# Squares of four head pairs folded by transfers and summed in one group of matmuls

## The chip, the cores and the metric

The kernel runs on one core of a Trainium2 chip. The metric is device time in microseconds (us) of one execution. A profiled execution lasts a little longer than its recorded span, since some work lies around the span.

## What is computed

A layer norm over 2048 tokens of 512 values is followed by two branches whose product is added to the input. The change touches the first one, an attention over four lags. Cut to what matters:

```python
q = _causal_dwconv(_silu(x @ Wq), conv_q_w)      # k and v likewise; 16 heads of 128
q = q * cos + rot_half(q) * sin                  # k likewise
q = q / jnp.maximum(jnp.linalg.norm(q, axis=-1, keepdims=True), 1e-12)
k = k / jnp.maximum(jnp.linalg.norm(k, axis=-1, keepdims=True), 1e-12)
for s in range(4):
    attn = jnp.einsum('bshd,bshd->bsh', q, _lag(k, s)) * scale
    out = out + (attn * sigmoid(_lag(a, s) * b))[..., None] * _lag(v, s)
```

Then out is divided by its root mean square over all heads, gated by silu(x @ Wz), and multiplied by Wout. The second branch is a feed-forward net with weights reduced to their signs. For the change only one thing has to be seen: per token and head, the kernel needs the sum over 128 channels of q squared and of k squared (the norms), and of q times k at four lags (the dots). Channels lie on partitions, so such a sum is a matmul by a matrix of zeros and ones.

## The kernel before, in words

Tokens come in four blocks of 512 (index b, 0 to 3), the 16 heads in eight pairs (index p, 0 to 7). A pair has 256 channels, laid out as two slices j of 128 partitions; in each slice partitions 0 to 63 belong to one head and 64 to 127 to the other.

`step(p, b)` (line 663) is the unit of work. For pair p it makes queries, keys and their products of block b+1, and values, gates and output of block b. TensorE does in it 8 matmuls each for q, k, v and z (`project`, line 339), and in every even p the output projection of the two pairs before (`output_projection`, line 616: four token chunks of four matmuls, the first two of each chunk for the earlier pair). Steps with b = -1 make block 0, with the feed-forward net's work in between. So blocks 1, 2 and 3 of the products are made in the steps with b = 0, 1 and 2.

In `products` (line 416), for pair p: ScalarE squares both slices of q and k into two tiles sq0 and sq1 (128 x 2 x 512, 512 KB each), and one accumulating DMA of GpSimd's queue adds sq1 to sq0 (line 435). VectorE multiplies q by the lagged k into tiles pr (128 x 4 x 512, 1 MB). In blocks 1 to 3 the dots of two pairs are brought into one tile. In an even p the second slice is added by DMA (line 452), then partitions 32 to 63 are added to 0 to 31, and 96 to 127 to 64 to 95, by two accumulating DMAs (line 469). In an odd p the pair's own tile goes into the free half of the tile of the pair before: two plain copies (line 472) and two accumulating DMAs onto them (line 473). The four dots of two pairs are then one group of four matmuls (`sum_dots`, line 494) with the matrix of_heads.

The squares are not brought together so. `sum_squares` (line 484) makes two matmuls for each pair (k and q) with of_head: even pairs write partitions 0 to 63 of the PSUM tile squares, odd pairs 64 to 127, so two pairs are four matmuls on four different groups of 32 columns. It is called at p = 2, 4 and 6 of a step between the second and third chunk of the output projection (`strips`, line 695) together with `sum_dots` of the last two pairs, and once more at p = 0 of the next block, before `norms` (line 505). `norms` adds both halves of the tile squares.

In `weighted` (line 569) the tiles te0 and te2 (one buffer each) hold coefficients times v; the output o stays in te0. In steps with b = 0 the squares of o go to te2 and from there to DRAM by a DMA of GpSimd's queue (line 599); in later steps they go through a free part of xnT. The tiles bc (three buffers) bring coefficients from DRAM by DMAs of SyncE's queue. `gated_output` (line 607) makes oz, which the output projection reads.

What goes through the wrapper InOrder (all TensorE and VectorE work, much of ScalarE's, the stores of line 599, the loads of bc) keeps its program order. DMAs issued by nc.gpsimd and nc.sync are placed into the queues of GpSimd and SyncE by the framework's scheduler when the kernel is built; from then on each queue runs in its order, and an instruction that waits holds up all behind it. GpSimd's queue carries the folds of sq and pr, the stores of parts of the output (lines 637 and 639), the accumulations of the next layer norm (line 241) and the stores of line 599. SyncE's carries all weights.

The tile pool holds sq0 in three buffers taken in turn, and sq1 in one.

Of the kernel before, what the change touches and what calls it, by code (L numbers as in the profile page):

```python
# [38 lines left out]
F32 = mybir.dt.float32  # L39
F32R = mybir.dt.float32r  # L40
AF = mybir.ActivationFunctionType
ALU = mybir.AluOpType
PSUM = bass.MemoryType.PSUM

P = 128
# [3 lines left out]
D = 128  # L49
# [4 lines left out]
NP = H // 2  # L54
TB = 512
# [26 lines left out]
def recurrent_layer(ctx: ExitStack, tc: tile.TileContext, a: dict, out: bass.AP):  # L82
    nc = tc.nc
# [12 lines left out]
    of_head = const.tile([P, NP, LW], F32, name="of_head")  # L96
# [3 lines left out]
    of_heads = const.tile([P, NP // 2, LW], F32, name="of_heads")  # L100
# [25 lines left out]
    qks = qk.enter_context(tc.tile_pool(name="qks", bufs=1))  # L126
# [174 lines left out]
    def load(pool, n, p, b):  # L301
        w = pool.tile([P, KC, 2 * P], F32, tag="w", name=f"w{n}{p}_{b}", bufs=3)
        loads["by"].dma_start(w, a[f"w{n}"][p])
        weights[n] = w
# [16 lines left out]
    def sum_with_halo(pool, name, p, b):  # L321

        if name in to_keep:
            to_keep.pop(name)()
        t = pool.tile([P, 2, HALO + TB], F32, tag=name, name=f"{name}_{p}_{b}", bufs=1)
        act.copy(t[:, :, 0:HALO], kept[name][:, p])
        if b < NTB - 1:
            to_keep[name] = lambda: act.copy(kept[name][:, p], t[:, :, TB : TB + HALO])
        return t
# [35 lines left out]
    def raw_of(pool, n, p, b, bufs=2, raw=None):  # L365

        raw = raw or with_halo(pool, f"r{n}", "raw", bufs, p, b)
        project(n, p, b, raw[:, :, HALO:])
        keep_halo(f"r{n}", raw, p, b)
        return raw  # L370

    def convolve(i, p, raw, to):

        for j in range(2):
            nc.scalar.mul(to[:, j, :], raw[:, j, HALO:], conv_w[:, i, p, j, LAGS - 1 : LAGS])  # L375
            for w in range(LAGS - 2, -1, -1):
                dve.scalar_tensor_tensor(
                    to[:, j, :],
                    raw[:, j, w : w + TB],
                    conv_w[:, i, p, j, w : w + 1],  # L380
                    to[:, j, :],
                    ALU.mult,
                    ALU.add,
                )

    banks = {}

    dots_due = []
    squares_due = []
    outputs_due = []  # L390

    def queries(p, b):

        if p or b:
            load(qks, "q", p, b)
        q = qks.tile([P, LAGS, 2, TB], F32, tag="q", name=f"q_{p}_{b}", bufs=1)
        q0 = q[:, LAGS - 1]
        convolve(0, p, raw_of(qks, "q", p, b), q0)
        return q

    def turn(q):
# [8 lines left out]
        for s in range(2, LAGS):  # L410
# [2 lines left out]
                q[:, at], q[:, at + 1], turns[:, 3:4], q[:, at + 2], ALU.mult, ALU.subtract  # L413
            )

    def products(p, b, q, between=None, beside_k=None):

        n = f"_{p}_{b}"
        if p or b:
            load(qks, "k", p, b)  # L420
        q0 = q[:, LAGS - 1]
        raw = raw_of(qks, "k", p, b)
        if p == 0:
            sum_squares(p)
        k = sum_with_halo(qks, "k", p, b)
        convolve(1, p, raw, k[:, :, HALO:])
        if between:
            between()
        turn(q)

        sq = [qks.tile([P, 2, TB], F32, tag=f"sq{j}", name=f"sq{j}" + n, bufs=3 - 2 * j) for j in range(2)]
        for j in range(2):
            act.activation(sq[j][:, 0], q0[:, j], AF.Square)
            act.activation(sq[j][:, 1], k[:, j, HALO:], AF.Square)
        nc.gpsimd.dma_start(sq[0], sq[1], accum_op=ALU.add)
        squares_due.append((p, sq[0]))
        if beside_k:
            beside_k()

        def product(to, j, lo, hi):  # L440

            k0 = k[:, j, lo : lo + TB]
            k_lags = bass.AP(k0.tensor, k0.offset, [k0.ap[0], [1, hi - lo], k0.ap[1]])
            dve.tensor_tensor(to, q[:, lo:hi, j, :], k_lags, ALU.mult)

        pr = qks.tile([P, LAGS, TB], F32, tag="pr", name="pr0" + n, bufs=2)
        product(pr, 0, 0, LAGS)
        if not b or p % 2 == 0:
            pr1 = qks.tile([P, LAGS, TB], F32, tag="pr", name="pr1" + n, bufs=2)
            product(pr1, 1, 0, LAGS)  # L450
            if b:
                nc.gpsimd.dma_start(pr, pr1, accum_op=ALU.add)
            elif p < NP - 1:
                dve.tensor_tensor(pr, pr, pr1, ALU.add)
        else:

            product(q[:, :, 1], 1, 0, LAGS)
            dve.tensor_tensor(pr, pr, q[:, :, 1], ALU.add)
        if not b:

            prs = [pr, pr1] if p == NP - 1 else [pr]
            dots_due.append([p, prs, of_head[:, p], p == NP - 1, True])
            return


        for h in range(0, P, D // 2):
            first, second = slice(h, h + D // 4), slice(h + D // 4, h + D // 2)
            if p % 2 == 0:
                nc.gpsimd.dma_start(pr[first], pr[second], accum_op=ALU.add)
            else:  # L470
                both = dots_due[-1][1][0]
                nc.gpsimd.dma_start(both[second], pr[first])
                nc.gpsimd.dma_start(both[second], pr[second], accum_op=ALU.add)
        if p % 2 == 0:
            dots_due.append([p, [pr], of_heads[:, p // 2], p == NP - 2, False])
        else:
            dots_due[-1][-1] = True

    def add(to, s, heads, src, start, stop):

        rows = to[LW * s : LW * s + LW, :]
        pe.matmul(rows, heads, src, start=start, stop=stop, tile_position=(0, LW * s))

    def sum_squares(last):


        while squares_due and squares_due[0][0] != last:
            p, sq = squares_due.pop(0)
            if p == 0:
                banks["squares"] = sums.tile([P, TB], F32, tag="squares", name="squares")  # L490
            for i in (1, 0):
                add(banks["squares"], 2 * (p % 2) + 1 - i, of_head[:, p], sq[:, i, :], p < 2, p >= NP - 2)

    def sum_dots():

# [48 lines left out]
    def squares_of_o():  # L544
        while o_due:
            o_due.pop(0)()
# [116 lines left out]
    def step(p, b, beside_q=None, beside_k=None):  # L663

        at = b >= 0
        change = p == 0 and at
        q = queries(p, b + 1)
        squares_of_o()
        if x_due:
            x_due.pop()()  # L670
        rv = with_halo(vs, "rv", "raw", 1, p, b) if p == b == 0 else None
        if beside_q:
            beside_q()
        if change and b:
            sum_squares(p)
            norms(b)
        due = bool(dots_due) and dots_due[0][-1]
        if change and not b:

            def beside_k():  # L680
                norms(b)
                norms_in_rows(b)

        products(p, b + 1, q, (lambda: norms_in_rows(b)) if change and b else None, beside_k)
        if z_due:
            z_due.pop()()
        if at:
            load(vs, "v", p, b)
            raw = raw_of(vs, "v", p, b, 1, rv)
        if first_due:  # L690
            first_due.pop()()
        if at:
            v = values(p, b, raw)

        def strips():

            if p and p % 2 == 0:
                sum_squares(p)
            if p == NP - 2 and b + 2 < NTB:
                gate_products(b + 2)  # L700
            if p == 1 and not at:
                gate_products(0)
            if due:
                sum_dots()

        z = []
        z_of = lambda: z.append(gates_of_output(p, b))

        early = p == 2 and b == 0
        if early:  # L710
            load(vs, "z", p, b)
            z_of()

        output_projections(strips if p % 2 == 0 or due else None)
        if change:
            coefficients(b)
        if at:
            if not early:
                load(vs, "z", p, b)
            load_wo(p, b)  # L720
            out_of = lambda: gated_output(p, b, weighted(p, b, v), z[0])
            if change:
                z_due.append(z_of)
                first_due.append(out_of)
            else:
                if not early:
                    z_of()
                out_of()
        if p == (3 if at else 2):
            load_gate(b + 1)  # L730
        elif p == (4 if at else 3):
            gate()
        if b + 2 < NTB:
            if p < TC:
                statistics(b + 2, p)
            if p == (TC if at else TC - 1):
                centre(b + 2)
            elif p == 5:
                divide(b + 2)
# [226 lines left out]
    with tc.tile_pool(name="ff", bufs=1, side="right") as ff:  # L966
# [75 lines left out]
        for b in range(1, NTB):  # L1042
# [31 lines left out]
            if b == last:  # L1074

                scale, silu, by_y, plus_x = ends(b, pf)
                n = len(hids)
# [97 lines left out]
```

## Time and profile before

| what | us |
|---|---|
| median of three runs | 1400.17 (1399.67 to 1402.85) |
| the profiled execution | 1400.38 |
| its span | 1398.6 |
| VectorE busy in it | 1179.3 |
| ScalarE busy in it | 671.3 |
| GpSimd busy in it | 236.1 |

The profile's page lists busy time of each engine, groups of instructions with their mean duration, and a chain of work followed back from the end. The trace can be asked for any stretch of the span: the timeline of one engine gives start, duration, operation, output and inputs of merged instructions and, in brackets, the idle time before the first of them with what ended it. Of float32 matmuls there are two records each, so that four matmuls are listed as x8. The issue of a DMA is a short record on its queue's engine; the time to landing is given apart. Times of the timelines count from the span's start. Windows give the mean busy share of the 16 DMA engines.

The times of GpSimd's transfers by the trace, over the whole span: the folds of sq (32 of 512 KB) land in 6.7 us in the median, the 72 small transfers of pr (256 KB) in 6.9 us, the 12 large ones (1 MB) in 10.7 us.

### The profile page before, as it was taken

The numbers are of one execution on the slowest core, as the hardware profiler recorded it, in microseconds if no ns is written. First come the engines' busy times: TensorE is split into PE (matmuls) and PEld (weight loads), VectorE is DVE, ScalarE is ACT, GpSimd is POOL, SyncE is SP. The second block draws the span as 40 slices with busy tenths as digits, with TensorE's granted clock in tenths as the row PEclk, the third lists the DMA queues.
The fourth block names the chain that finished last, engine by engine and source line by source line (L and its number), as shares of the span: only waits on it lengthen the run. The fifth ranks groups of instructions, "written<-read, shape, count | busy, mean of one in ns | idle before, by whom it ended". The sixth has DMA issues, their size and how long they took to land.

```text
span 1398.6 us, 12500 instructions
## 1 busy us (share of the span) xinstructions
PE 1387.6 (99%) x3962; PEld 689.6 (49%) x3962; DVE 1179.3 (84%) x1183; ACT 671.3 (48%) x1309; POOL 236.1 (17%) x317
## 2 busy tenths in 40 slices
PE   9999999999999999999999999999999999999998
PEld 6555544444444444444444444444444444578886
DVE  7998989999898989998999999989884987337454
ACT  7566656546454564565545544545442433222122
POOL 2222111112213121113131112111111122200000
PEclk9999999999999999999999999999999999999999
DMA  9979577888988789889986897888849999654020
GB/s 315 332 171 211 129 200 166 228 203 197 231 199 186 167 167 242 212 211 196 212 186 159 171 251 186 207 181 182 176 92 207 262 233 237 142 204 136 24 90 30
DMA packets 104985, 263.40 MB, mean 188 GB/s; under 512 B 17812, under 2 KB 18324, under 8 KB 100568
## 3 DMA queue, kind: packets, MB, share of 16 engines
q0 software_dynamic: 36672, 108.02, 40.0%
q1 hardware_dynamic: 68248, 154.58, 37.1%
q8 instruction: 32, 0.52, 0.2%
q14 instruction: 33, 0.27, 0.1%
HBM read 159.77 MB, written 52.45 MB: 152 GB/s over the span
## 4 chain that ended last, share of the span: by engine, by line
PE 87%; DVE 7%; DMA 3%; ACT 1%; issue 1%; SPq 0%; DVEq 0%; ACTq 0%
PE pq L76 14%; PE pk L76 14%; PE po L76 14%; PE pz L76 13%; PE pv L76 12%; PE ph L76 8%; PE pf L76 8%; DVE q L76 2%; DVE te L76 2%; DMA wk<-in_wk_dram 1%; DVE v L76 1%; PE dots L76 1%; DMA bc<-co_dram 1%; PE squares L76 1%; DVE k L76 1%
## 5 line engine op out<-in xcount | busy, mean ns | idle before, releaser
L76 PE MATMUL pq<-xnT,wq 128*128 128x512 f32 (+1 forms) x528 | 226.1, 580 | 0.6 <-ACT rk L310 0.6
L76 PE MATMUL pk<-xnT,wk 128*128 128x512 f32 x512 | 225.3, 592 | 0.8 <-DMA wk<-in_wk_dram 0.8
L76 PE MATMUL pz<-xnT,wz 128*128 128x512 f32 x512 | 225.2, 592 | 0.5 <-ACT rv L363 0.5
L76 PE MATMUL po<-wo,oz 128*128 128x512 f32 x512 | 225.6, 595 | 0.0
L76 PE MATMUL pv<-xnT,wv 128*128 128x512 f32 x512 | 225.2, 592 | 0.0
L76 DVE TENSOR_TENSOR te<-v,bc 128x2048 f32<-128x2048 f32 x64 | 143.8, 2288 | 33.8 <-ACT v L76 15.8
L76 DVE SCALAR_TENSOR_TENSOR k<-rk,conv_w,k 128x512 f32<-128x512 f32 x192 | 141.7, 751 | 31.6 <-ACT k L375 27.1
L76 PEld LDWEIGHTS pq<-xnT,wq 128*128 128x128 f32 x528 | 99.0, 189 | 123.4 <-issue 115.1
L76 PEld LDWEIGHTS po<-wo,oz 128*128 128x128 f32 x512 | 96.2, 190 | 126.5 <-issue 117.1
L76 PEld LDWEIGHTS pz<-xnT,wz 128*128 128x128 f32 x512 | 96.6, 189 | 124.0 <-issue 119.2
L76 PEld LDWEIGHTS pv<-xnT,wv 128*128 128x128 f32 x512 | 96.6, 189 | 123.8 <-issue 120.2
L76 PEld LDWEIGHTS pk<-xnT,wk 128*128 128x128 f32 x512 | 96.5, 189 | 121.7 <-issue 119.6
L76 DVE SCALAR_TENSOR_TENSOR q<-rq,conv_w,q 128x512 f32<-128x512 f32 x192 | 141.5, 749 | 17.4 <-ACT q L375 10.6
L76 DVE SCALAR_TENSOR_TENSOR v<-rv,conv_w,v 128x512 f32<-128x512 f32 x192 | 141.3, 750 | 6.4 <-ACT v L375 1.9
L76 DVE SCALAR_TENSOR_TENSOR q<-q,turns 128x1024 f32<-128x1024 f32 (+1 forms) x128 | 127.3, 1015 | 4.9 <-ACT q L76 2.6
L76 DVE TENSOR_TENSOR pr<-q,k 128x2048 f32<-128x2048 f32 x52 | 117.3, 2287 | 0.9
L76 DVE CAST hid_hi<-hid 128x512 fp32r<-128x512 f32 x52 | 22.4, 430 | 89.7 <-ACT hid L785 89.7
L785 ACT ACTIVATE hid<-ph,up_scale 128x512 f32<-128x512 f32 x64 | 43.6, 685 | 108.6 <-PE ph L76 108.0
L363 ACT ACTIVATE rq<-pq 128x512 f32<-128x512 f32 x62 | 36.9, 596 | 98.2 <-PE pq L76 98.1
L633 ACT COPY part<-po 128x512 f32<-128x512 f32 x64 | 37.0, 580 | 87.8 <-PE po L76 87.7
L76 PE MATMUL ph<-xs_hi,up 128*128 128x512 f32 x192 | 76.8, 400 | 0.0
L76 PE MATMUL ph<-xs_lo,up 128*128 128x512 f32 x192 | 75.6, 394 | 0.0
(154 smaller groups left out, 1747.2 us busy)
## 6 DMA issues: line engine op xcount, KB each, us to landing
bc<-co_dram SPq DMA_DIRECT2D x128, 256.0 KB
pr<-pr POOLq DMA_DIRECT2D x72, 256.0 KB, 6.9
wq<-in_wq_dram SPq DMA_DIRECT2D x32, 512.0 KB
wk<-in_wk_dram SPq DMA_DIRECT2D x32, 512.0 KB
sq<-sq POOLq DMA_DIRECT2D x32, 512.0 KB, 6.7
wv<-in_wv_dram SPq DMA_DIRECT2D x32, 512.0 KB
wz<-in_wz_dram SPq DMA_DIRECT2D x32, 512.0 KB
wo<-in_wo_dram SPq DMA_DIRECT2D x32, 512.0 KB
```

What stands on the lines that cost most here:

```text
L76: return self.tc.keep_in_program_order(getattr(self.engine, op)(*args, **kwargs))
L363: nc.scalar.activation(to[:, j, :], pp, AF.Silu)
L633: nc.scalar.copy(part, po)
L785: nc.scalar.activation(hid, ph, AF.Relu, scale=scale)
```

## The change

The folding of a pair's tile is moved into a helper `beside`, which serves pr as before, and now sq too, for pairs 0 to 3 of blocks 1 to 3. There, after sq1 has been added to sq0, an even pair's tile is folded by two accumulating DMAs of 128 KB; an odd pair's tile goes into the free half of the tile of the pair before by two plain copies and two accumulating DMAs of 128 KB. Pairs 0 to 3 then take two entries in place of four, both summed at p = 4 with of_heads; the call at p = 2 is left out in the steps with b >= 0. Pairs 4 to 7 and block 0 are summed as before. The three buffers of sq0 have tags of their own, and each pair is given one by hand.

```diff
+    def beside(p, of_pair, both):
+        for h in range(0, P, D // 2):
+            first, second = slice(h, h + D // 4), slice(h + D // 4, h + D // 2)
+            if p % 2 == 0:
+                nc.gpsimd.dma_start(of_pair[first], of_pair[second], accum_op=ALU.add)
+            else:
+                nc.gpsimd.dma_start(both[second], of_pair[first])
+                nc.gpsimd.dma_start(both[second], of_pair[second], accum_op=ALU.add)
...
-        sq = [qks.tile([P, 2, TB], F32, tag=f"sq{j}", name=f"sq{j}" + n, bufs=3 - 2 * j) for j in range(2)]
+        place = (2, 0, 1, 0, 0, 2, 1, 0)[p] if b else p % 3
+        sq = [
+            qks.tile([P, 2, TB], F32, tag=tag, name=f"sq{j}" + n, bufs=1)
+            for j, tag in enumerate((f"sq_{place}", "sq1"))
+        ]
...
         nc.gpsimd.dma_start(sq[0], sq[1], accum_op=ALU.add)
-        squares_due.append((p, sq[0]))
+        if not b or p >= NP // 2:
+            squares_due.append((p, sq[0], of_head[:, p], p % 2, p < 2, p >= NP - 2))
+        else:
+            beside(p, sq[0], squares_due[-1][1] if p % 2 else None)
+            if p % 2 == 0:
+                squares_due.append((p, sq[0], of_heads[:, p // 2], p // 2, True, False))
...
-            p, sq = squares_due.pop(0)
+            p, sq, heads, odd, start, stop = squares_due.pop(0)
...
-                add(banks["squares"], 2 * (p % 2) + 1 - i, of_head[:, p], sq[:, i, :], p < 2, p >= NP - 2)
+                add(banks["squares"], 2 * odd + 1 - i, heads, sq[:, i, :], start, stop)
...
-            if p and p % 2 == 0:
+            if p and p % 2 == 0 and not (at and p == 2):
                 sum_squares(p)
```

How the built queues differ: TensorE has 12 matmuls less and is otherwise in the same order, VectorE's order is the same. GpSimd has 36 DMAs more, each set right behind the sq fold of its pair and so ahead of that pair's transfers of pr. On SyncE two weight loads stand earlier: wk of pair 4 of block 1 stands ahead of the second half of bc of pair 3, the loads of the gate and one of x, where it stood behind them; wv of pair 4 in the step with b = 1 likewise. ScalarE has a few small moves in the same places.

More of the change, by code (lines that the diff above doesn't have):

```diff
@@ L463, in products @@
             return
[L466 to L473, printed above, removed]
+        beside(p, pr, dots_due[-1][1][0] if p % 2 else None)
         if p % 2 == 0:
```

## The prediction

> **What bounds the kernel now.** I read the page's busy times first, then the chain of waits, then timelines of single engines around the edit.
>
> ```profile
> span 1398.6 us, 12500 instructions
> PE 1387.6 (99%) x3962; PEld 689.6 (49%) x3962; DVE 1179.3 (84%) x1183; ACT 671.3 (48%) x1309; POOL 236.1 (17%) x317
> ```
>
> TensorE idles 11 us in all. The timeline of PE has no gap between 335.7 and 1089 us, so a matmul taken out there is time won, and a wait put in is time lost. Step p=4, b=0, where pairs 0 to 3 of block 1 will be summed:
>
> ```profile
> 342.60 7.03 PE L76 MATMUL po<-wo,oz 128*128 128x512 f32 x16
> 349.56 1.06 PE L76 MATMUL squares<-sq,of_head 128*32 128x512 f32 x8
> 350.44 1.04 PE L76 MATMUL dots<-pr,of_heads 128*32 128x512 f32 x8
> 351.42 7.13 PE L76 MATMUL po<-wo,oz 128*128 128x512 f32 x16
> ```
>
> See the starts, not the durations: the four square matmuls take 350.44 - 349.56 = 0.88 us of PE, since they run side by side on four column groups.
>
> The last stall before the gapless stretch, by the chain and by PE's timeline:
>
> ```profile
> 299.01 2.30 DVE te L76
> 301.31 0.02 issue
> 301.33 7.01 DMA bc<-co_dram
> ...
> 308.40 20.25 DMA wk<-in_wk_dram
> ```
> ```profile
> 328.79 7.11 PE L76 MATMUL pk<-xnT,wk 128*128 128x512 f32 x16 [0.80 <-DMA wk<-in_wk_dram]
> ```
>
> And GpSimd's queue in step p=3, b=0:
>
> ```profile
> 318.73 0.86 POOL L435 DMA_DIRECT2D sq<-sq  x1 [8.96 <-ACT sq L76]
> 328.42 1.04 POOL L472 DMA_DIRECT2D pr<-pr  x2 [8.82 <-DVE pr L76]
> 335.72 0.79 POOL L473 DMA_DIRECT2D pr<-pr  x1 [6.27 <-DMA pr<-pr]
> 339.74 0.78 POOL L473 DMA_DIRECT2D pr<-pr  x1 [3.23 <-DMA pr<-pr]
> ```
>
> By the times to landing the sq fold took 9.4 us, the two last transfers 12.1 and 9.5 us: the dots' operand is whole at 339.74 + 9.5 = 349.2, and PE reads it at 350.44. That is 1.2 us of slack, and the edit puts new transfers ahead of these four lines.
>
> **Matmuls removed.** Twelve at a mean of 592 ns would be 7.1 us, but they overlap. One group costs 349.56 to 350.44 = 0.88; at p=6 the starts of squares, ab and dots (420.29, 421.18, 422.04) give 0.89 and 0.86. One group of two goes in each of three blocks: 3 x 0.87 = 2.6 us. The dots group stays at p=2, so the switch between tile shapes around it (7.13 in place of 7.03 for the next po) stays too.
>
> **Loads moved.** On SyncE's queue wk of pair 4 now stands ahead of bc, gates and x. Its buffer comes free when pq of pair 3 ends (about 300.4), so it issues some 8 us earlier than 308.40; even with 20.25 us to land it is there at 321 for a use at 328. The 0.80 us stall goes. What is late next is oz of pair 3: VectorE has no idle time from 263 to 342, oz ends at 342.07, and PE wants it two matmuls into the po of 342.60, at about 344.3. Slack 2.2 us, of which 0.87 + 0.80 would be used. bc gets the extra wait of one issue and is read 30 us later: nothing. In b=1 wv moves from 585.86 to at the earliest 578.6 (the end of pz), and bc behind it waits for VectorE until 580.95 anyway: nothing.
>
> **Transfers added.** 36 DMAs of 128 KB, 12 per block. Their issue is 0.5 to 0.8 us each by L472/L473, about 25 us on a GpSimd busy 236 us: no bound. What counts is that copy and accumulate wait for landings, with everything behind them held.
>
> *Even pairs.* In p=2 the fold of 286.97 lands in 4.6 us at 291.6, the two half folds are out by 293.2, and the pr fold waits for VectorE until 294.80: nothing. In p=0 of block 1 the same (213.78 + 6.9 = 220.7, pr at 226.04). In p=0 of block 2 498.83 + 6.6 makes pr 1.7 us late, with the next sq at 523.42 free again.
>
> *p=1, b=0.* sq fold 242.06, lands in 7.7: 249.8. Two copies of 128 KB: no row has them; 256 KB took 4.9 here, I take 4.3 (bounds 3 and 5): 254.2 and 254.8. Accumulates out by 255.9. pr copies at 256.0 in place of 252.22, 5.0 to land, pr accumulates out by 262.8, so the store of te2 (queued behind) issues at 262.9 in place of 261.93. With its 7.3 us it lands at 270.2; VectorE rewrites te2 at 269.86. The added 0.5 MB comes on top: the software queue's 108 MB took 40% of the span, 5.2 us a MB, so up to 2.6 us where the DMA engines are full (shares 1.05, 1.03, 1.11 from 246 to 264). VectorE waits 0.3 to 3 us, I take 1.5. PE's po of 277.70 wants oz only two matmuls in and has 2.3 us: hidden. But VectorE stays late to 342, where only 2.2 - 1.67 = 0.6 was left, so PE waits 0.9 there.
>
> *p=3, b=0.* This is the term that decides. sq squares 1.5 late (they follow VectorE): fold 320.2, +9.4 = 329.6. Copies 5 us (bounds 3.5, the 256 KB rows of the later blocks, and 8.8, this step's own row): 335.2. Accumulates out at 336.1. pr copies 336.2 and 336.7 in place of 328.42; they land in 3.5 to 8.8, I take 6, since 336 to 342 has a DMA share of 0.64: 342.7. Last accumulate issues at 343.5; landing 7 to 12.1, I take this step's 9.5, as 342 to 360 is full (1.07 to 1.10): 353.0. The optimistic ends give 348, the pessimistic 358. PE arrives at 350.44 - 1.67 + 0.9 = 349.7 and waits 3.3 us. Against before, dots start 353.0 - 350.44 = 2.6 us later. Behind them stand the rest of po and the whole gapless stretch; nothing takes it back. What GpSimd has queued behind (layer-norm accumulations, part stores) has its users 20 us or more away. ScalarE rewrites the buffer of pair 3's squares at 347.64, which the accumulates leave at about 344: 3 us to spare.
>
> *Blocks 2 and 3.* p=3, b=1: 599.98 + 9.9 = 609.9, copies 3.6, accumulates out 615, pr copies 615.1 in place of 610.13, +3.6, accumulates out 620.1, +6.9 = 627; dots at 634.56. 7 us free. b=2 (882.71, +9.5; dots 918.68) is alike, and p=1 of both leaves 5 us or more. Nothing, and each keeps its 0.87.
>
> **A rule against the row.** The Trainium skill, "DMA: Bandwidth & Descriptors", section "Anatomy of one DMA", puts a transfer at about 2.0 us plus its bytes over 436 GB/s: 3.2 us for the sq fold, 2.3 for each of 128 KB, 2.6 for 256 KB. The p=3 chain would then be 320.2 + 3.2 + 2.3, pr copies at 328.4 as now, and the dots' operand there at 335: no wait, and the change would win the whole 3.4 us. The rows say 9.4 and 12.1 for the same kinds, because the engines are shared with the loads of weights. I take the rows.
>
> **Sum** on the profiled execution (1400.38; the median is 0.21 below, inside the runs' spread): +2.6 at the dots of block 1 (with the first group and the 0.80 swallowed by it) - 2 x 0.87 = +0.9, so 1401.3.
>
> **Rivals.**
> 1. *The wait eats the gain* (above): operand whole at 350 to 354.8, 1398.9 to 1403. Chance 0.45.
> 2. *The transfers are hidden*: they land by 349.7, since wk's 512 KB now moves before 320 and frees the engines from 318 on. Then -2.6 - 0.8 = -3.4, 1397.0, up to 1398.8 with some wait for VectorE. For it: landings of 3.5 in later blocks. Against: 9.4 to 10.0 for every sq fold of odd pairs but one of 7.7 and one of 8.8. Chance 0.23, 0.14 of it below 1397.4.
> 3. *Slower: GpSimd's chain in p=3, b=0 at its slow rows.* From a landing after 354.8 the loss (4.4 - 1.7) is over 0.2%; at 357 it is 6.6 - 1.7 = +4.9, 1405.3. For it: 8.8 and 12.1 were seen in this very step, and a late VectorE delays its start. Chance 0.24.
> 4. *Traffic*: 4.7 MB more at 5.2 us is 24 us of full DMA time, and weight loads elsewhere come late; a few stalls like that of 0.80 would give 1404. Against: no such wait now after 335. Chance 0.08.
>
> That the matmuls saved count in full (7.1 us, 1393) contradicts the starts above; 0.01 or less.
>
> About 0.2% (2.8 us) is what a measurement of this kernel can tell from no change. Faster by more: 0.14 (part of 2). Slower: 0.24 + 0.06 + 0.05 of case 1's upper end. Same: 0.51. The range 1397.0 to 1406.0 leaves out the ends of 2 and of 3; case 1's own is 1398.9 to 1403.0.
>
> **What would show it.** In the profile after: squares gone at p=2 and po to po there about 0.98 us apart; no wait for wk at 328; pr copies of pair 3 some 8 us after the sq fold's landing; PE waiting before the dots of pairs 2 and 3 of block 1, named as a DMA of pr; none in blocks 2 and 3, whose spacing of p=2 shrinks by 0.87. I am wrong if the dots of block 1 wait for nothing, if blocks 2 or 3 wait as well, or if the store of te2 doesn't hold up VectorE near 270 yet oz is late.

## The result and the profile after

The changed kernel takes 1423.07 us in the median of five runs (1422.68 to 1424.81), the kernel before in the same session 1401.58 (1399.67 to 1402.85): 1.0157 times as long, 95% interval 1.0143 to 1.0172. The profiled execution lasted 1423.62 us, so 23.2 more than the one of before. The forecast was 1401.3, its range ended at 1406.0.

The page of the changed kernel, first the span with the busy times, then the first line of the chain that ended last:

```profile
span 1421.8 us, 12490 instructions
...
PE 1390.8 (98%) x3938; PEld 690.0 (49%) x3938; DVE 1179.6 (83%) x1183; ACT 671.3 (47%) x1309; POOL 261.7 (18%) x353
...
PE 74%; DMA 10%; DVE 9%; issue 3%; ACT 2%; POOL 1%; SPq 0%; DVEq 0%; POOLq 0%; ACTq 0%
```

TensorE has 24 records (12 matmuls) less and yet is busy 3.2 us longer; its idle time has gone from 11 to 31 us. The waits of TensorE, with us in total, times, and the longest:

```profile
PE dots L76 <- DMA pr<-pr: 11.8, 2, 10.8
PE po L76 <- DVE oz L76: 6.2, 1, 6.2
PE pz L76 <- ACT rv L363: 2.4, 1, 2.4
```

None of the first two stood in the profile before; the third had 0.5 us there. TensorE's timeline in the steps p=2 and p=4 with b=0 puts the two long waits into block 1:

```profile
278.03 1.88 PE L76 MATMUL po<-wo,oz 128*128 128x512 f32 x4
286.10 8.12 PE L76 MATMUL po<-wo,oz 128*128 128x512 f32 x12 [6.19 <-DVE oz L76]
294.14 1.06 PE L76 MATMUL dots<-pr,of_heads 128*32 128x512 f32 x8
...
358.59 1.05 PE L76 MATMUL squares<-sq,of_heads 128*32 128x512 f32 x4 [0.39 <-DMA sq<-sq]
370.41 1.94 PE L76 MATMUL dots<-pr,of_heads 128*32 128x512 f32 x8 [10.76 <-DMA pr<-pr]
372.27 7.71 PE L76 MATMUL po<-wo,oz 128*128 128x512 f32 x16
```

The squares are gone at p=2 (only the dots stand between the chunks of po), and the dots of p=4 start at 370.41 where they started at 350.44. In blocks 2 and 3 one wait of 1.01 us is left (the dots of block 2's pairs 2 and 3, at 656.34). Why block 1 is late, GpSimd's queue tells, first p=1, then p=3, both b=0:

```profile
251.51 1.03 POOL L424 DMA_DIRECT2D sq<-sq  x2 [7.96 <-DMA sq<-sq]
258.34 0.79 POOL L425 DMA_DIRECT2D sq<-sq  x1 [5.80 <-DMA sq<-sq]
...
260.15 1.28 POOL L424 DMA_DIRECT2D pr<-pr  x2
267.30 0.78 POOL L425 DMA_DIRECT2D pr<-pr  x1 [5.87 <-DMA pr<-pr]
...
270.23 0.60 POOL L76 DMA_DIRECT2D o_dram<-te  x1
```
```profile
327.72 0.86 POOL L452 DMA_DIRECT2D sq<-sq  x1 [8.17 <-ACT sq L76]
338.67 1.04 POOL L424 DMA_DIRECT2D sq<-sq  x2 [10.09 <-issue]
344.36 1.61 POOL L425 DMA_DIRECT2D sq<-sq  x2 [4.65 <-DMA sq<-sq]
345.71 1.28 POOL L424 DMA_DIRECT2D pr<-pr  x2
360.74 0.79 POOL L425 DMA_DIRECT2D pr<-pr  x1 [13.75 <-DMA pr<-pr]
362.02 0.77 POOL L425 DMA_DIRECT2D pr<-pr  x1 [0.50 <-DMA pr<-pr]
```

Read the starts downwards: where a bracket names a DMA, the queue waits for a transfer issued one or two lines above. The fold of p=3 waits for ScalarE's squares, and the copies behind it (the trace names no releaser for them) leave about 1.4 us after the fold has landed (327.72 + 9.6). In p=1 the store of te2 leaves at 270.23 and lands 8.6 us later, at 278.8. That is when VectorE may rewrite te2; its line of this kernel, and the same line in the run with the fold in block 1 alone:

```profile
278.84 2.29 DVE L76 TENSOR_TENSOR te<-v,bc 128x2048 f32<-128x2048 f32 x1 [8.58 <-DMA bc<-co_dram]
```
```profile
284.26 2.29 DVE L76 TENSOR_TENSOR te<-v,bc 128x2048 f32<-128x2048 f32 x1 [10.63 <-DMA o_dram<-te]
```

In the first the trace names a load of bc, in the second the store; that it is the store in both is shown below, where moving the store alone ends the wait. The rest of VectorE's step follows, oz is late, and po waits 6.19. In p=3 the copies of pr leave at 345.71 in place of 328.42. Half of these 17.3 us is VectorE's lateness (its last product for them ends at 337.10 in place of 328.12), half the squares' chain ahead of them. They then take 14.7 and 15.3 us to land, so that the last accumulation lands at about 370.3, when the dots start.

Windows of the changed kernel (us from and to, length, busy time of PE, PEld, DVE, ACT and POOL, the clock granted to TensorE as a share of full speed, DMA share, GB/s) show a third cost, the clock after the stall:

```profile
282.00:286.00 4.00, 0.00 (x0) 0.00 (x0) 3.86 (x4) 1.71 (x3) 0.00 (x0) 0.84 0.00 0
286.00:290.00 4.00, 3.90 (x5) 1.84 (x6) 3.86 (x7) 2.53 (x4) 0.87 (x1) 0.50 0.67 102
290.00:294.00 4.00, 4.00 (x8) 1.40 (x7) 3.89 (x6) 3.39 (x6) 0.57 (x1) 0.80 0.15 29
```

TensorE resumes at 286.10, but for some 5.5 us at half its clock (0.50 until 290, and a mean of 0.80 in the next 4 us is 1.6 us more at half): in 286 to 290 it has 5 records, where four-us windows at full clock have some 11. The 12 records of po took 8.12 us instead of the 5.42 that twelve take at full clock; after the second stall the dots took 1.94 instead of 1.04 and po 7.71 instead of 7.13: 4.2 us together.

The account of the 23.2 us: waits 6.19 + 0.39 + 10.76 + 1.01, the longer one for rv (2.41 - 0.46) and 0.3 more for the first wq make 20.6; slow matmuls 4.2; groups saved -2.6, the stall for wk gone -0.8 (pk of 336.45 waits for nothing). That is 21.4. Of the 1.8 us that are left, 1.2 lie in p=4: the dots start 13.26 us after the squares (357.15, 370.41) where it was 0.88, so 12.4 more, of which the two waits there are 11.15; the second half of the squares waited for its transfer and ran alone, no longer beside the first. 0.6 us are not placed.

### The profile page after: what moved, and what is told of

Read it like the earlier page. It is cut to its first block, busy times and chain, and to the rows that moved or that the text cites. A ratio compares the mean times of both kernels' runs of the same rounds, so it can differ in the third digit from the quotient of the medians.

```text
span 1421.8 us, 12490 instructions
## 1 busy us (share of the span) xinstructions
PE 1390.8 (98%) x3938; PEld 690.0 (49%) x3938; DVE 1179.6 (83%) x1183; ACT 671.3 (47%) x1309; POOL 261.7 (18%) x353
## 4 chain that ended last, share of the span: by engine, by line
PE 74%; DMA 10%; DVE 9%; issue 3%; ACT 2%; POOL 1%; SPq 0%; DVEq 0%; POOLq 0%; ACTq 0%
PE pq L76 12%; PE po L76 12%; PE pk L76 12%; PE pz L76 11%; PE pv L76 10%; PE ph L76 8%; PE pf L76 8%; DMA pr<-pr 5%; DVE te L76 2%; DVE q L76 2%; DMA sq<-sq 2%; DVE k L76 1%; PE dots L76 1%; DMA bc<-co_dram 1%; DVE v L76 1%
## 5 line engine op out<-in xcount | busy, mean ns | idle before, releaser
L76 PE MATMUL po<-wo,oz 128*128 128x512 f32 x512 | 229.1, 602 | 6.2 <-DVE oz L76 6.2
```

The lines of the kernel that those rows point to most:

```text
L76: return self.tc.keep_in_program_order(getattr(self.engine, op)(*args, **kwargs))
```

## The experiments

Theories at the start. **Queue**: the loss is the place of the squares' transfers on GpSimd's queue, ahead of pr and of te2's store, each waiting for a landing. **Traffic**: 4.7 MB more on DMA engines that are already full. Later the question became why delayed copies of pr take 15 us. Ratios are to the kernel before in runs on the same chip, with 95% intervals.

**The fold in block 1 alone, and in blocks 2 and 3 alone.**

```diff
+        folded = b in (1,)
...
-        if not b or p >= NP // 2:
+        if not folded or p >= NP // 2:
...
```

> The fold of squares by transfers in block 1 of the products alone; blocks 2 and 3 summed as before. Queue theory (in the steps with b=0 the transfers ahead of those of pr hold up the store of te2 and the dots; blocks 2 and 3 have slack): nearly the whole loss stays, the two waits of PE before po of p=2 and before the dots of p=4 are there again, and the two groups saved elsewhere are gone: 1422 to 1425. Traffic theory (each block's extra bytes make weights and coefficients late): about a third of the loss, 1408.

1423.8 us (1419.89 to 1430.14), ratio 1.0144 (1.0121 to 1.0167). The profile, of the longest run, has both waits: 11.7 us for oz and 10.6 before the dots.

The other half has `b in (2, 3)`:

> The fold in blocks 2 and 3 alone. Queue theory: 2 x 0.87 us saved, up to 1 us of waiting for the dots of block 2 (1.01 in the changed kernel, which came to that point later): 1399 to 1401, no change that can be told. Traffic theory: two thirds of the loss, about 1415.

1405.16 us (1399.41 to 1415.34), ratio 1.0025 (1.0009 to 1.0041). Block 1 makes the whole loss by itself, with half as many bytes added as blocks 2 and 3 together. The two blocks lose 0.25% with a wide scatter, more than the queue theory had (a gain) and far less than traffic had. The profiled run (1401.35) shows no wait at the dots, so what the longer runs wait for is not seen.

**Interleaved.** An odd pair's squares are copied right behind their fold, then pr is copied, and only then come the accumulations, so that no landing of squares stands whole ahead of pr's copies. All bytes stay.

```diff
+                    pool.dma_start(sq_too[0][second], sq_too[1][first])
...
+                    if i == 0:
+                        pool.dma_start(to[second], src[first])
+            for to, src in ([] if sq_too is None else [sq_too]) + [(both, of_pair)]:
...
+                    pool.dma_start(to[second], src[second], accum_op=ALU.add)
```

> All transfers of the change, in another order: in odd pairs the two copies of squares are issued right after the fold, then the two copies of pr, and only then the accumulates of both, so that nothing of pr is held up by the landing of a copy of squares. Queue theory: the pr copies of pair 1 of block 1 issue at about 253 in place of 260 and those of pair 3 some 6 us earlier than in the changed kernel; the store of te2 still is 1 to 3 us late, the dots wait a few us at most: 1400 to 1408. Traffic theory: as the changed kernel, 1420 to 1425.

1407.65 us (1401.27 to 1416.35), ratio 1.005 (1.0033 to 1.0067). GpSimd's timeline at p=3, b=0 of this kernel:

```profile
336.27 1.05 POOL L76 DMA_DIRECT2D sq<-sq  x2 [9.79 <-issue]
337.29 1.00 POOL L76 DMA_DIRECT2D pr<-pr  x2
341.21 1.60 POOL L76 DMA_DIRECT2D sq<-sq  x2 [2.92 <-DMA sq<-sq]
342.82 1.59 POOL L76 DMA_DIRECT2D pr<-pr  x2
```

The copies of pr follow those of sq by 1 us, not 7, and have landed within 5.6; the dots wait for nothing. Two thirds of the loss go with no byte removed. In its profile po still waits 4.04 us for oz, and VectorE had waited 3.84 us in p=0 for the norms' rows (rk<-r), perhaps behind the half folds of the even pair.

**An eighth of the bytes.** The added transfers move 64 of 512 columns, in the order of the change; the other columns stay unfolded.

```diff
-            beside(p, sq[0], squares_due[-1][1] if p % 2 else None)
+            some = lambda t: None if t is None else t[:, :, 0:64]
+            beside(p, some(sq[0]), some(squares_due[-1][1]) if p % 2 else None)
```

> The changed kernel with each added transfer cut to 64 of 512 columns (16 KB in place of 128 KB); most columns of the squares of pairs 0 to 3 are then not folded. Number, order and waits of the transfers are the same. If the bytes moved set their landing, they land in 2 to 3 us in place of 5 to 7 and the time falls to 1402 or below. If the place in the queues of the DMA engines behind other transfers sets it, they land about as late as before and the loss stays within a few us: 1415 to 1423.

1414.61 us (1412.94 to 1418.09), ratio 1.0091 (1.0073 to 1.0109). Some 13 of 21 us stay with 16 KB transfers: the two issued at 340.47 took 10.7 and 12.3 us to land, where those of 128 KB at the same place took 10.6 and 13.2. A small transfer is no quick one here. The other 8 us went with the bytes.

**Interleaved, and the first store of te2 by SyncE.** To see whether po's 4.04 us belong to the store.

```diff
-                pool.dma_start(o2_dram[b], o2)
+                (pool if b else sp).dma_start(o2_dram[b], o2)
```

> The interleaved order (all transfers kept), and the store of the squares of o of pair 0, block 0, issued by SyncE, so that GpSimd's queue no longer holds back the freeing of te2. Queue theory: the wait of PE before the po of p=2, b=0 (4.04 us in the interleaved kernel's profile, and the slow matmuls behind it) goes: 4 to 6 us less than the interleaved kernel, 1400 to 1403. If something else than the store made VectorE late there, no gain: 1407.

1405.69 us (1400.94 to 1407.34; two runs of seven near 1401, the others above 1405.6), ratio 1.0021 (1.0003 to 1.0038). The wait for oz at p=2 is gone; a wait of 2.21 before the dots has come, and it too is followed by half the clock, by TensorE's timeline and a window of this run:

```profile
352.87 1.72 PE L76 MATMUL dots<-pr,of_heads 128*32 128x512 f32 x8 [2.21 <-DMA pr<-pr]
```
```profile
354.00:356.00 2.00, 2.00 (x6) 0.84 (x3) 1.96 (x2) 0.00 (x0) 0.37 (x1) 0.50 1.10 222
```

What separates the two groups of times is open.

**The changed kernel with that store by SyncE** (the same two lines):

> The changed kernel, with the first store of te2 issued by SyncE, and all else as in it. Takes away the wait of PE before the po of p=2, b=0 (6.2 us, and 3 us of slow matmuls behind it), but not the wait before the dots of p=4. If the two add up: 1413 to 1416. If PE only comes earlier to the dots and waits there for longer: 1420 to 1423.

1417.56 us (1415.25 to 1418.7), ratio 1.011 (1.0096 to 1.0123). VectorE doesn't wait for te2, po doesn't wait at p=2, and the dots wait 11.22 us, much as in the changed kernel: the two waits add up. The store's place is worth 5.5 us in the medians, 1.6 short of the range given for that case, and the rest stays with pr's chain. GpSimd's timeline at p=3, b=0, with VectorE on time:

```profile
327.71 1.04 POOL L424 DMA_DIRECT2D sq<-sq  x2 [8.43 <-DMA sq<-sq]
...
336.24 1.30 POOL L424 DMA_DIRECT2D pr<-pr  x2
349.82 0.79 POOL L425 DMA_DIRECT2D pr<-pr  x1 [12.28 <-DMA pr<-pr]
351.34 0.78 POOL L425 DMA_DIRECT2D pr<-pr  x1 [0.72 <-DMA pr<-pr]
```

The copies of pr leave at 336.24 and take 13.3 and 14.3 us, so the long landing does not need the stall of p=1.

**The layer norm's store in larger pieces.** Delayed to 345.71, pr's copies stand behind a store of statistics that SyncE had issued 5.2 us ahead of them. In the run above they were 5.1 us behind it too. In the kernel before they stood 3.1 us ahead of it (328.42 and 331.48), in the interleaved order 2.0 us. SyncE's timeline of the changed kernel:

```profile
340.47 0.38 SPq L238 DMA_DIRECT2D ln_dram<-ln  x1
...
343.94 1.23 SPq L76 DMA_DIRECT2D bc<-co_dram  x2
```

It writes 2 KB in pieces of 4 bytes. In the experiment the pieces have 16 bytes.

```diff
-            nc.sync.dma_start(ln_dram[b][i].rearrange("(c p) -> p c", p=P), ln[:, i, :])
+            nc.sync.dma_start(ln_dram[b][i].rearrange("(p c) -> p c", p=P), ln[:, i, :])
```

> The changed kernel; the means and deviations of a layer norm are stored to DRAM in 128 pieces of 16 bytes in place of 512 of 4 (their order in DRAM is then another one, so tokens get each other's means). Asks why the pr copies of pair 3 of block 1 took 15 us to land. If the small pieces of this store, issued 5 us before, clog the queues, they land in 7 to 9 us and the time falls by 5 to 8 us: 1415 to 1418. If not, 1422 to 1424 with landings of 14 to 16.

1417.55 us (1414.15 to 1422.32), ratio 1.0117 (1.0088 to 1.0145). DMA packets and queues in the window from 344 to 350, first of the changed kernel, then of this one:

```profile
DMA packets 227, 0.39 MB, mean 64 GB/s; under 512 B 53, under 2 KB 53, under 8 KB 227
q1 hardware_dynamic: 212, 0.34, 81.3%
q0 software_dynamic: 15, 0.04, 3.3%
```
```profile
DMA packets 443, 1.17 MB, mean 195 GB/s; under 512 B 62, under 2 KB 62, under 8 KB 420
q1 hardware_dynamic: 324, 0.72, 54.2%
q0 software_dynamic: 118, 0.44, 37.7%
```

With the small pieces the packets of q1 hold 81% of the engines' time for 0.34 MB and GpSimd's queue (q0) gets 3%; with the larger ones q0 moves eleven times as much. (This run is 1.7 us ahead of the other there; in its window as far behind the store, 342.3 to 348.3, q0 has 0.23 MB, six times as much.) The copies of pr land in 9.6 and 10.5 us instead of 15, and the wait before the dots is 7.14, so 3.6 us less. The median is 5.5 us lower, but po's wait at p=2, which lies ahead of this store, is shorter too in this profile (4.7). The same edit in the kernel before:

> The kernel before with the layer norm's store in pieces of 16 bytes (tokens get each other's means), as the measure for the run of the changed kernel with it. Its dots of block 1 had 1.2 us of slack and waited for nothing, so nothing is to be won: 1399 to 1402.

1400.69 us (1399.15 to 1406.1), ratio 0.9994 (0.9984 to 1.0004): there the store harms nobody who is waited for. The slow stretch itself is there as well: 51 and 87 GB/s in the windows 333 to 337 and 337 to 341 of the kernel before, 111 and 208 with the larger pieces.

**Broadcast loads from other rows.** bc spreads single rows over 64 partitions; if that reading caused the slow stretch, reading different rows would end it.

```diff
-                row = co_dram[b][lo : lo + 2, 2 * p + h, :]
+                rows_of = co_dram[b].rearrange("s r t -> (s r) t").rearrange("(p i) t -> p i t", i=2)
...
-                    bc[h * D // 2 : (h + 1) * D // 2], row.partition_broadcast(D // 2)
+                    bc[h * D // 2 : (h + 1) * D // 2], rows_of
```

> The changed kernel; each load of bc reads 128 different rows of the same coefficients (as many bytes) in place of two rows read 64 times, so the coefficients are wrong ones. If reading one row 64 times makes these loads slow and all transfers behind them late, the pr copies of pair 3, issued 2 us after such a load, land in about 7 us in place of 15, and the wait before the dots is at most 4 us in place of 10.8: 1405 to 1414. If the loads do no more than any other of 256 KB: 1422 to 1424.

1418.77 us (1415.22 to 1423.14), ratio 1.0123 (1.009 to 1.0156); in its profile pr's copies still took 12.7 and 13.4 us and the dots waited 10.38. In the kernel before:

> The kernel before with the same altered loads of bc (wrong coefficients), as the measure for the run of the changed kernel with them. TensorE has no waits to lose, so by either theory 1399 to 1401.

1400.03 us (1398.52 to 1403.27), ratio 0.9991 (0.9984 to 0.9998). The reading of single rows accounts for 2 us of pr's landing at most. The changed kernel got 4.3 us faster all the same, and po waits 3.93 in this profile. As that wait lies between 3.1 and 11.7 in the profiles that have te2's store behind the squares in the change's order, medians of four runs can't tell this gain from the 5.5 us of the larger pieces; what speaks for the pieces is the landings and the wait before the dots.

**Interleaved, store by SyncE, and even pairs' half folds behind the large fold of pr.**

```diff
-                nc.gpsimd.dma_start(pr, pr1, accum_op=ALU.add)
+                pool.dma_start(pr, pr1, accum_op=ALU.add)
+                if halves:
+                    beside(p, sq[0], None)
```

> All of the change in blocks 1 to 3, with the interleaved order in odd pairs, the first store of te2 by SyncE, and in even pairs the half folds of squares issued behind the fold of pr, so that in p=0 of block 1 they no longer run beside the eight small loads of rq and rk, for which VectorE waited 4.0 us in the interleaved kernel's profile. Queue theory: no transfer of pr issues more than 3 us later than in the kernel before; the waits go, the scatter of the interleaved kernel's runs (1401 to 1416) shrinks, 1398 to 1402. Traffic theory: the bytes are all there, 1405 or more.

1410.04 us (1406.15 to 1411.73), ratio 1.0056 (1.0042 to 1.007): a miss. The copies of pair 3's pr leave at 332.39 and 333.90, the last accumulation at 346.51 (before: 339.74), and the dots wait 2.59. The second copy, 0.8 us ahead of the layer norm's store, took 12.3 us. The squares' copies and accumulations still stand ahead of pr's; the run after the next takes them away from there.

The same order in blocks 2 and 3 alone, block 1 as before:

> The same order, in blocks 2 and 3 alone, with block 1 as in the kernel before. Two groups of matmuls saved, nothing held up: 1.7 us less than before, 1398 to 1400; if the traffic alone costs, 1403 to 1406 as the kernel with the fold in blocks 2 and 3 in the order of the change.

1400.98 us (1399.22 to 1403.91), ratio 0.9997 (0.9987 to 1.0006). No loss, but no gain of 1.7 either. The profile has waits of 1.08 for q (pk) and 0.40 at the dots, which the one of before lacks.

**All of pr ahead of the squares.** For odd pairs: copies of pr, copies of sq, accumulations of pr, accumulations of sq; the rest as in the last but one.

```diff
+            some = [(both, of_pair)] if sq_too is None else [(both, of_pair), tuple(t for t in sq_too)]
...
+            for to, src in some:
...
+                    pool.dma_start(to[second], src[first])
+            for to, src in some:
...
+                    pool.dma_start(to[second], src[second], accum_op=ALU.add)
```

> All folds of squares kept, but behind the dots' operand in GpSimd's queue: for odd pairs pr copies, then sq copies, then pr accumulates, then sq accumulates; for even pairs the half folds behind the large pr fold; the first store of te2 by SyncE. If the place in the queue is all of block 1's loss, pr copies of pair 3 issue near 328.5 as before, the dots wait for nothing, and the time is 1398 to 1401.5 (2.6 of matmuls saved, less about 1.5 for the late store of te2). If what stayed in the order tried before (1410) is the price of the added bytes, it stays here too: 1405 to 1410, with landings of pr copies and accumulates longer by some us.

1403.74 us (1401.19 to 1408.92), ratio 1.0016 (1.0009 to 1.0024). GpSimd's timeline of this kernel:

```profile
330.74 1.04 POOL L76 DMA_DIRECT2D pr<-pr  x2 [8.82 <-DVE pr L76]
331.76 0.49 POOL L76 DMA_DIRECT2D sq<-sq  x1
...
337.98 1.68 POOL L76 DMA_DIRECT2D pr<-pr  x2 [4.23 <-DMA pr<-pr]
339.68 0.77 POOL L76 DMA_DIRECT2D sq<-sq  x1
```

The copies of pr wait for VectorE alone, as before the change, and the dots of block 1 for nothing. With all its bytes the loss is down from 21.5 to 2.5 us, short of the 1398 to 1401.5 that the queue theory had. The same with transfers of an eighth:

> The same order, with the added half folds, copies and accumulates of squares cut to 64 of 512 columns (16 KB each; most columns of the squares then miss their second half). Place theory: as the kernel with full transfers, within 1.5 us. Byte theory: 3 to 7 us less than that kernel.

1403.88 us (1401.57 to 1409.4), ratio 1.0022 (1.0013 to 1.0031): no difference, so in this order the bytes cost nothing that can be measured. And with the layer norm's store in larger pieces:

> The same order with full transfers, and the layer norm's store in 128 pieces of 16 bytes per half in place of 512 of 4 bytes (its values land in another order). If pr's accumulates of pair 3 still lie in the slow stretch behind that store, their landing shortens from 9 to 12 us to 6 to 8 and a wait before the dots of up to 3 us goes: 1 to 4 us less than with the plain store. If no wait is there, no difference.

1405.83 us (1402.35 to 1409.3), ratio 1.0025 (1.0013 to 1.0037): no gain, and none was to be had where nothing waits at the dots.

## Why the prediction was wrong

**The mechanism was named, its size was not.** Rival 3 (GpSimd's chain in p=3, b=0) is what happened, but it was given 1405.3, and the stall of p=1, which the sum had as hidden, came on top. The steps in order:

- *Matmuls removed, loads moved*: right. The groups are gone and the 0.80 us for wk too.
- *"p=1, b=0 ... VectorE waits 0.3 to 3 us, I take 1.5 ... hidden"*: failed. The store of te2 was to leave at 262.9; it left at 270.23. The copies of 128 KB were taken at 4.3 us by scaling down a row of 256 KB; 251.51 to 258.34 is 6.8. The copies of pr then took 6.9 and 8.5 us in place of 5.0, in a stretch that the new transfers share. The store took 8.6 in place of 7.3. VectorE waited 8.58, not 1.5, and of this 6.19 reached po, which was held to be hidden. Moving only the store to SyncE gave 5.5 us back (1423.07 to 1417.56).
- *"p=3, b=0 ... This is the term that decides ... they land in 3.5 to 8.8, I take 6"*: failed most. The sq fold was later by 7.5 us than forecast (327.72 against 320.2), most of it the 7.1 us that VectorE had waited beyond the forecast; the fold's landing (9.6) and that of the copies (5.4 to 5.7) were as forecast. But the copies of pr were costed from rows of transfers that went ahead of the layer norm's store. At 345.71 they went behind it, and took 15. At the forecast's own time, 336.2, they would have gone behind it too: with te2's store on SyncE they left at 336.24, took 13.3 and 14.3 us in place of 6, and the last accumulation left at 351.34 in place of 343.5. This landing is the term that was mis-sized. Larger pieces in that store bring 15 to 10 and take 3.6 us off the wait. The landing of the dots' operand was put at 353.0, with 358 for the pessimistic end; it was 370.3. What else keeps pr's copies at 10 us in that stretch, was not tried.
- *Not in the sum at all*: the clock. The Trainium skill, "TensorE: Matmul & The Clock Gate", section "Part 1: The HAM clock gate", has the array fall to half clock after about 3.4 us of idleness and come back after about 3.4 us of work. The windows above agree in kind: 0.50 after a stall of 6.19, and full clock again some 5.5 us later. As to how much idleness it takes, the runs differ from the page: the clock was at 0.50 after waits of 2.21 (shown above) and, with the half folds behind pr's large fold, 2.59, while the wait of 2.41 for rv in the changed kernel left it at 1.00. So the forecast's own wait of 3.3 us should have had a price beyond itself; the real ones cost 4.2 us.
- *p=0, "the same: nothing"*: not safe. In the profiles of the block 1 fold alone and of the interleaved order VectorE waited 4.00 and 3.84 us for rk<-r behind the half folds, in that of the changed kernel 0.19, and 0.20 in the interleaved order with the store on SyncE; that the half folds are the cause is not shown.
- *Blocks 2 and 3*: nearly right. One wait of 1.01 in block 2, which the prediction had named as a sign of being wrong, and no measurable loss when the order there is mended; a gain of two groups isn't measurable either.
- *Traffic* (rival 4): ruled out as the main cause. The order, with te2's store on the other queue, took the loss from 21.5 to 2.5 us with every byte kept, and cutting the bytes in that order changed nothing. In the order of the change the bytes did matter: an eighth of them took 8 of the 21 us away.

Open: the last 2.5 us of the best order with block 1 in it, and the scatter of the fold in blocks 2 and 3. In the profile of that order po waits for oz twice, 2.5 us in all (VectorE's te still waited 1.68 for the store some 70 us ahead of the first), and a product of the feed-forward net waits 3.7 for VectorE in a step long after. That profile is of a run of 1408.67, 4.9 above the median, so it may show more than the median has; which of these makes the median was not tried. No version with the fold was faster than the kernel before.

## What to carry to other kernels

A transfer added to an in-order queue, with another that waits for it, costs those behind them a whole landing (an eighth of the bytes still lost 13 of 21 us here), and what it delays must be costed at its new time, next to what it will then run beside. Before saving 0.9 us of an engine, compare the slack of the shared queue (here 1.2 us) with the delay put into it (pr's copies left 18.0 us behind the sq fold in place of 9.7); if the transfers must go there, put them behind the ones that somebody waits for. A stall of TensorE of 6 us cost 2.7 us more than itself here, since the work after it ran at half clock.

## What the runs showed of the hardware that was not expected

- Landing hardly followed size on these busy engines. At the same place, the accumulations of squares in p=3, 16 KB took 10.7 and 12.3 us and 128 KB 10.6 and 13.2. Copies of 256 KB took 6.9 and 8.5 us in p=1 and 14.7 and 15.3 in p=3.
- One store of 512 pieces of 4 bytes (340.47) was followed by 8 us, from 342 to 350, in which the 16 engines moved 46 and 82 GB/s and GpSimd's queue almost nothing (0.04 MB in 344 to 350); with pieces of 16 bytes it moved 0.23 MB as far behind the store.
- The granted clock fell to 0.50 during the stalls of 6.19 and 10.76 us and stayed there for the next 5.5 and 3 us of work. A stall of 2.21 us was followed by 0.50 as well.
